# Cross-attention's mask carried in the last feature row of its keys, with the query weights folded on TensorE

## The chip, the core and the metric

The kernel runs on one core of a Trainium2 chip, as one launch. The metric is the device time of that launch in microseconds (us). The text calls the engines by the profile's names: PE (TensorE matmuls; PEld is its weight load), DVE (VectorE), ACT (ScalarE), POOL (GpSimd) and SP (SyncE, which here only issues DMAs).

## The reference

Four blocks run one after the other on x of shape (8, 256, 128) and ctx_512 of shape (8, 64, 64). L0 is a gated cross-attention, L1 a cross-attention with a residual, L2 six layers of a decoder, L3 a cross-attention whose softmax runs over the queries. L2 takes nearly all of the time, and the change is in it:

```python
H, D, FF, L = 16, 64, 512, 6            # heads, head size, hidden size, layers

def _ln(x, g, b, eps=1e-05):
    m = jnp.mean(x, axis=-1, keepdims=True)
    v = jnp.mean(jnp.square(x - m), axis=-1, keepdims=True)
    return (x - m) / jnp.sqrt(v + eps) * g + b

def _mha(s, t, kv_w, q_w, o_w, o_b, mask):
    k, v = jnp.split(s @ kv_w, 2, axis=-1)
    q = t @ q_w
    k, v, q = (_heads(k), _heads(v), _heads(q))
    scores = jnp.einsum('bhqd,bhkd->bhqk', q, k) * D ** (-0.5)
    scores = jnp.where(mask[:, None] == 0, jnp.float32(-1000000000.0), scores)
    attn = jax.nn.softmax(scores, axis=-1)
    o = jnp.einsum('bhqk,bhkd->bhqd', attn, v)
    ...
    return o @ o_w + o_b

def step(t, p):                          # one layer; t is (8, 256, 128)
    tn = _ln(t, norm_g, norm_b)
    t = _mha(tn, tn, skv, sq, sow, sob, tgt_mask) + t      # mask (8, 256, 256)
    tn = _ln(t, norm_g, norm_b)
    t = _mha(src, tn, ckv, cq, cow, cob, src_mask) + t     # src = ctx_512, mask (8, 1, 64)
    tn = _ln(t, pg, pb)
    return t + (jax.nn.relu(tn @ w1 + b1) @ w2 + b2), None
```

The cross-attention's mask has one row of 64 keys per batch element, the same for every head and query. norm_g and norm_b (128 values each) are the same in all layers.

## The kernel before

All of x stays in SBUF as `t`, tokens on the partitions. Work is written as steps that are put into a plan with `at(tick, phase, fn)`. At the end the steps run in order of tick and phase, and a dependency between successive instructions of PE, DVE, ACT and POOL pins each engine to that order; DMAs on SP are issued in program order. Matmul results and scores go through a rotation of four PSUM buffers of two banks each (`two_banks`, `mm_tile`, `tp_tile`); the n-th taker waits until the (n-4)-th is read out.

A layer has 32 ticks of self-attention (four per batch element b) and then 16 ticks of cross-attention (two per b, one for each half, `qt`, of the queries). The feed-forward of a b comes some ticks behind its cross-attention.

- `ahead` prepares a b's normalised input: moments on DVE, rstd on POOL, xn (on ACT at L868 if `on_scalar`, else on DVE at L873), a transpose on PE (L882), and an ACT copy to `tT` that multiplies by the column `g` and adds the column `bias` (L884; features are on the partitions there). For self-attention and cross-attention the two columns are norm_g and norm_b. Self-attention passes `on_scalar=False`.
- `plan_sa` does self-attention: projections (L902, L921), scores (L939), the exponent's input with the mask on DVE (L953), exp on ACT (L958), division on POOL (L968), transposes on DVE (L978), values (L994), output projection (L1012), addition into t (L1019).
- `plan_ca_weights` turns a layer's cross-attention weights once. It transposes w_ckv and w_cq on DVE in blocks of 32 (L1057), stores each to DRAM in four DMAs and fetches it back, regroups the first on POOL (L1074), and folds them into `AT` (keys' weights by query weights, L1083 on PE, copied by ACT) and `WVO` (values' weights by output weights, same lines).
- `plan_ca` makes the keys of two b's at once from `AT` and the context (`keys_both`: L1120 on PE, four copies on ACT, L1126). The keys are laid out as features on 128 partitions by 16 heads by 64 keys. Its scores are in `plan_weights_64`.
- `plan_weights_64` is shared with L0. For cross-attention, `scores` issues four times four matmuls of the keys (L356), and behind each four of them four bf16 matmuls that add the mask by a row of ones (L363). `lower` then copies to SBUF on ACT (L372), takes the maximum on DVE (m, L374) and subtracts it on POOL (L375); `exps` is on ACT; `divide` sums on DVE (L385) and multiplies on POOL (L387); `turn` transposes on DVE (L395); `sums` multiplies by the values on PE (L429); `add` adds into t on DVE (L1145).

These calls place the steps of `plan_ca_weights`; its `T` is six ticks ahead of the layer's cross-attention:

```python
        for i in range(2):
            at(T - 6 + i, 8.7, lambda i=i: turned(i))
            at(T - 4 + i, -0.5, lambda i=i: fetched(i))
        at(T + 1, 8.05, regrouped)
        at(T + 2, 3.6, folded("AT", 0, lambda c: st[1][:, :, c, :], HD ** -0.5))
        at(T + 3, 3.6, folded("WVO", 1, lambda c: W["ca", l][2][:, c, :]))
```

Of the kernel before, what the change touches and what calls it, by code (L numbers as in the profile page):

```python
# [8 lines left out]
F32 = mybir.dt.float32  # L9
I32 = mybir.dt.int32  # L10
BF16 = mybir.dt.bfloat16
# [16 lines left out]
def tile_xattn_stack(ctx: ExitStack, tc: tile.TileContext, io, out: bass.AP):  # L28
# [28 lines left out]
    def big(tag, bufs=4, shape=(P, 1024), dtype=F32):  # L57

        return heap.tile(list(shape), dtype, tag=tag, name=uniq(tag), bufs=bufs)
# [202 lines left out]
        return nm  # L262


    nm2 = const.tile([P, B, M], BF16, tag="nm2", name="nm2")
    nc.vector.memset(nm2, 0.0)
    ones0 = const.tile([P, 32], BF16, tag="ones0", name="ones0")
    nc.vector.memset(ones0, 0.0)
    nc.vector.memset(ones0[0:1], 1.0)


    def stats(xin, eps):
# [21 lines left out]
    def at(tick, phase, fn):  # L294
        plan.setdefault(tick, []).append((phase, fn))
# [30 lines left out]
        )  # L326
        return vw

    def plan_weights_64(tick, qt, qT, keys, values, mask, take):

        tl = {}

        def scores():
            sc = two_banks("sc").rearrange("p (q x) -> p q x", q=4)
            if mask is None:
                for i in range(4):
                    for a in range(4):
                        q = (i + 2 * (a // 2)) % 4  # L340
                        rows = slice(64 * (a // 2), 64 * (a // 2) + 64)
                        qb = 4 * qt + q
                        nc.tensor.matmul(
                            sc[32 * a : 32 * a + 32, q, :],
                            lhsT=qT()[rows, qb * 32 : (qb + 1) * 32],
                            rhs=keys()[rows, 4 * (a % 2) : 4 * (a % 2) + 4, :].rearrange(
                                "p h k -> p (h k)"
                            ),
                            start=True, stop=True,
                        )  # L350
                tl["sc"] = sc.rearrange("p q x -> p (q x)")
                return
            for q in range(4):
                qb = 4 * qt + q
                for a in range(4):
                    nc.tensor.matmul(  # L356
                        sc[32 * a : 32 * a + 32, q, :],
                        lhsT=qT()[:, qb * 32 : (qb + 1) * 32],
                        rhs=keys()[:, a].rearrange("p h k -> p (h k)"),
                        start=True, stop=False,  # L360
                    )
                for a in range(4):
                    nc.tensor.matmul(  # L363
                        sc[32 * a : 32 * a + 32, q, :], lhsT=ones0, rhs=mask,
                        start=False, stop=True,
                    )
            tl["sc"] = sc.rearrange("p q x -> p (q x)")

        def lower():
            sc = tl.pop("sc")  # L370
            e = big("e", shape=(P, 16, M))
            nc.scalar.copy(e.rearrange("p h k -> p (h k)"), sc)  # L372
            m = sm([P, 16], "m16")
            nc.vector.tensor_reduce(m, e, AX.X, ALU.max)  # L374
            nc.gpsimd.tensor_tensor(  # L375
                e, e, m.unsqueeze(2).to_broadcast([P, 16, M]), ALU.subtract
            )
            tl["e"] = e

        def exps():  # L380
            nc.scalar.activation(tl["e"], tl["e"], AF.Exp)

        def divide():
            r = sm([P, 16], "r16")
            nc.vector.tensor_reduce(r, tl["e"], AX.X, ALU.add)  # L385
            nc.vector.reciprocal(r, r)  # L386
            nc.gpsimd.tensor_tensor(  # L387
                tl["e"], tl["e"], r.unsqueeze(2).to_broadcast([P, 16, M]), ALU.mult
            )

        def turn():
            e = tl.pop("e").rearrange("p (q h) (k x) -> p (h k) q x", q=4, x=32)
            eT = big("k" if mask is None else "o", shape=(P, 8, 4, 32))
            for i in range(2):
                nc.vector.transpose(eT[:, 4 * i : 4 * i + 4], e[:, 4 * i : 4 * i + 4])  # L395
            tl["eT"] = eT

        def sums_by_head():

            ps = two_banks("mm").rearrange("p (i x) -> p i x", i=2)  # L400
            eT, vw = tl.pop("eT"), values()
            for i in range(2):
                for k in range(2):
                    for j in range(4):
                        nc.tensor.matmul(
                            ps[32 * j : 32 * j + 32, i, :P],
                            lhsT=cones.rearrange("p a f -> p (a f)") if i == 0
                            else vw[:, 4 * k + j, :],
                            rhs=eT[:, 2 * j + k].rearrange("p q x -> p (q x)"),
                            start=(k == 0), stop=(k == 1),  # L410
                        )
            r = sb([P, P], "r0", 2)
            nc.vector.reciprocal(r, ps[:, 0, :P])
            tl["oT"] = sb([P, P], "o0", 3)
            nc.vector.tensor_tensor(tl["oT"], ps[:, 1, :P], r, ALU.mult)

        def outputs():
            ps = mm_tile()
            nc.tensor.matmul(
                ps[:, :D], lhsT=tl.pop("oT"), rhs=S0["wo"], start=True, stop=True  # L420
            )
            take(ps)

        def sums():
            ps = mm_tile()
            eT, vw = tl.pop("eT"), values()
            for s in range(8):
                g, r, k = s // 4, s // 2 % 2, s % 2
                nc.tensor.matmul(  # L429
                    ps[:, :D], lhsT=eT[:, s].rearrange("p q x -> p (q x)"),  # L430
                    rhs=vw[:, r, k, g, :], start=(s == 0), stop=(s == 7),
                )
            take(ps)

        at(tick, 1, scores)
        at(tick, 2, lower)
        if mask is None:
            at(tick + 1, 2.05, exps)
            at(tick + 1, 2.5, turn)
            at(tick + 2, 1.9, sums_by_head)  # L440
            at(tick + 2, 4.6, outputs)
        else:
            at(tick, 8, exps)
            at(tick + 1, 2.4, divide)
            at(tick + 2, 2.5, turn)
            at(tick + 3, 3.0, sums)
# [188 lines left out]

    def mask_keys():
        mi = big("q", dtype=I32)
        mi = mi[0:1, : B * M].rearrange("p (b m) -> p b m", b=B)
        nc.sync.dma_start(out=mi, in_=io["mask_Bx1xS2_if1"].rearrange("b o m -> o b m"))
        nc.vector.tensor_scalar(nm2[0:1], mi, 0.0, -BIG, ALU.is_equal, ALU.mult)  # L640

    mask_bf = []

# [39 lines left out]
    def plan_l0(b, T):  # L683
# [87 lines left out]
        at(T + 1, 3.2, make_values)  # L771
        for qt in range(QT):
            plan_weights_64(
                T + qt, qt, lambda: st["q"], lambda: st["k"], lambda: st["VW"], None,
                lambda ps, qt=qt: add(qt, ps),
            )
        at(T + 3, 6, moments)
# [113 lines left out]
    def plan_sa(l, b, T):  # L891
# [134 lines left out]
        def mask():  # L1026
            st["nm"] = load_mask(b)

        ahead(b, (T - 6, 8.3), (T - 5, 2.6), (T - 5, 7.2), norm_g, norm_b, st, False)
        at(T - 2, -1, mask)  # L1030
        at(T - 4, 3.6, lambda: project(W["sa", l][2], "q", HD ** -0.5, 0, False))
        at(T - 4, 3.7, lambda: project(W["sa", l][2], "q", HD ** -0.5, 1, False))
# [13 lines left out]
    def plan_ca_weights(l, T):  # L1046
# [19 lines left out]
        def fetched(i):  # L1066
            w = W["ca", l][i]
            nc.sync.dma_start(out=w, in_=W.pop(("cab", l, i)).rearrange("j b i x -> (j b) (i x)"))
            st[i] = w.rearrange("p (i c x) -> p i c x", i=4, x=32)
# [26 lines left out]
                st[name] = res  # L1096
            return fn

        for i in range(2):
            at(T - 6 + i, 8.7, lambda i=i: turned(i))  # L1100
            at(T - 4 + i, -0.5, lambda i=i: fetched(i))
        at(T + 1, 8.05, regrouped)
        at(T + 2, 3.6, folded("AT", 0, lambda c: st[1][:, :, c, :], HD ** -0.5))
        at(T + 3, 3.6, folded("WVO", 1, lambda c: W["ca", l][2][:, c, :]))

    keys_of = {}

    def plan_ca(l, b, T):
# [3 lines left out]
        def keys_both():  # L1112
# [16 lines left out]
                    )  # L1129
            keys_of[b], keys_of[b + 1] = res  # L1130

        def make_values():
            st["VW"] = values_of(b, fold["WVO"])

        def res():
            st["tb"] = residual(b, W["ca", l][3])

        ahead(b, (T - 4, 6), (T - 3, 2.95), (T - 2, 2.9), norm_g, norm_b, st)
        if b % 2 == 0:
            at(T - 2, 3.7, keys_both)  # L1140
        at(T + 2, 3.2, make_values)
        at(T + 2, 7, res)

        def add(qt, ps):
            nc.vector.tensor_add(t[:, QT * b + qt, :], ps[:, :D], st["tb"][:, qt, :])  # L1145

        for qt in range(QT):
            plan_weights_64(
                T + qt, qt, lambda: st["tT"], lambda: keys_of[b], lambda: st["VW"],
                nm2[:, b].unsqueeze(1).to_broadcast([P, 4, M]), lambda ps, qt=qt: add(qt, ps),  # L1150
            )

    def plan_ff(l, b, T, T_second, steps=None):
# [117 lines left out]
    for l in range(NL):  # L1271
        T_ca = T0 + 4 * B
        T_next = T_ca + 2 * B
        for b in range(B):
            plan_sa(l, b, T0 + 4 * b)
        plan_ca_weights(l, T_ca - 6)
        for b in range(B):
            plan_ca(l, b, T_ca + 2 * b)
            T_ff = T_ca + 2 * b + 7
# [101 lines left out]
```

## Time and profile before

| | before |
|---|---|
| median of 3 runs | 2409.77 us (2405.57 to 2410.28) |
| profiled execution | 2410.29 us, of which the profile's span is 2408.5 |
| granted TensorE clock, mean | 0.987 |
| instructions | 100346 |
| busy: PE, DVE, ACT, POOL | 2325.2, 1872.3, 1707.7, 1359.1 us |
| chain that ended last | PE 75%, DVE 13%, ACT 5%, POOL 4% |
| L356, L363 (cross-attention's scores, mask) | 217.0 us busy in 3072, 112.4 in 1536 |
| DMA | 76.90 MB, mean 32 GB/s |

A busy share is an average over stages with different limits, and matmuls overlap, so a busy time of PE is more than the time by which it delays what follows. In the rows of the groups, the columns are line, engine, operation, output <- inputs, shape, count, then busy us and mean ns of one, then idle time of the engine just before and what ended it. In a timeline, the columns are start and duration in us, engine, line, operation, count; a bracket gives the engine's idle time before it and what released it.

### The profile page before, as it was taken

Reading aid. Unit: us, or ns where it says so; the run is one execution under the profiler, and the core shown is the slowest. Engines: PE = TensorE matmul, PEld = TensorE weight load, DVE = VectorE, ACT = ScalarE, POOL = GpSimd, SP = SyncE. Lnnn points to the kernel's source line nnn. Section 1 sums busy time; section 2 is a strip of 40 time slices with the busy share of each in tenths; the row PEclk is TensorE's granted clock in tenths of the full one; section 3 lists DMA queues with packets and bytes.
Section 4 is the critical chain, followed back from the end, with each engine's and each line's share of the span. In section 5 each row is a group of like instructions: output and inputs, shape, how many; then the busy total and the mean of one; then the engine's idle time right before and its main releaser. Section 6 shows DMA issues by size and latency. Waiting matters only on the chain.

```text
span 2408.5 us, 100346 instructions
## 1 busy us (share of the span) xinstructions
PE 2325.2 (97%) x42564; PEld 1719.9 (71%) x42564; DVE 1872.3 (78%) x6237; ACT 1707.7 (71%) x4514; POOL 1359.1 (56%) x2231
## 2 busy tenths in 40 slices
PE   7889999999999999999999999999999999999997
PEld 4557777777777777777777777777777777777775
DVE  5677887777888767888767888767888767888775
ACT  4567777667777667778667778667778667777663
POOL 2444556754556754555764555755555765455665
PEclk9989999999999999999999999999999999999998
DMA  6000022001022001012000012000013000001000
GB/s 180 2 2 20 21 73 65 2 3 30 21 64 66 11 3 30 21 56 73 12 2 26 21 45 87 12 2 18 25 40 89 21 2 18 25 26 42 2 4 16
DMA packets 102834, 76.90 MB, mean 32 GB/s; under 512 B 8113, under 2 KB 96881, under 8 KB 102386
## 3 DMA queue, kind: packets, MB, share of 16 engines
q1 hardware_dynamic: 101794, 70.16, 10.1%
q8 instruction: 335, 5.49, 0.9%
q14 instruction: 113, 0.93, 0.1%
q10 hardware_dynamic: 592, 0.33, 0.1%
HBM read 62.07 MB, written 8.39 MB: 29 GB/s over the span
## 4 chain that ended last, share of the span: by engine, by line
PE 75%; DVE 13%; ACT 5%; POOL 4%; issue 2%; DMA 0%; SPq 0%; POOLq 0%; ACTq 0%; DVEq 0%
PE sc L939 12%; PE mm L902 12%; PE mm L994 12%; PE mm L1012 6%; PE mm L921 6%; PE mm L429 6%; PE sc L356 5%; DVE e L953 3%; PE mm L1178 3%; PE mm L1161 3%; DVE eTc L978 2%; DVE m L374 2%; POOL e L968 2%; PE mm L1120 2%; PE mm L318 2%
## 5 line engine op out<-in xcount | busy, mean ns | idle before, releaser
L968 POOL TENSOR_SCALAR e<-e,rs 128x256 f32<-128x256 f32 x1536 | 702.8, 478 | 706.3 <-DVE rs L966 696.5
L958 ACT ACTIVATE e<-e,mn 128x256 f32<-128x256 f32 x1536 | 758.6, 495 | 151.3 <-DVE mn L953 146.5
L953 DVE CUSTOM_DVE_ANT_0 e<-sc,nm 128x256 f32<-128x256 f32 x1536 | 543.1, 419 | 93.4 <-PE sc L939 92.3
L978 DVE STREAM_TRANSPOSE eTc<-e 128x512 f32<-128x512 f32 x768 | 516.2, 694 | 59.4 <-POOL e L968 58.2
L939 PE MATMUL sc<-k,q 64*32 64x256 f32 x12288 | 380.8, 383 | 2.3 <-DVE o L299 1.3
L994 PE MATMUL mm<-eTc,v 32*64 32x256 f32 x12288 | 363.4, 378 | 5.7 <-ACT AT L1095 3.3
L375 POOL TENSOR_TENSOR e<-e,m 128x1024 f32<-128x1024 f32 x112 | 213.0, 1902 | 262.1 <-DVE m L374 262.1
L994 PEld LDWEIGHTS mm<-eTc,v 32*64 32x64 f32 x12288 | 277.1, 131 | 88.5 <-issue 22.2
L939 PEld LDWEIGHTS sc<-k,q 64*32 64x32 f32 x12288 | 221.8, 107 | 125.3 <-issue 51.4
L374 DVE TENSOR_REDUCE m<-e 128x16 f32<-128x1024 f32 x112 | 136.3, 1217 | 197.0 <-ACT e L372 197.0
L958 ACT ACTIVATION_READ_ACCUMULATOR e<-e,mn 128x1 f32 x1536 | 287.9, 187 | 0.0
L356 PE MATMUL sc<-q,tT 128*32 128x256 f32 x3072 | 217.0, 382 | 3.8 <-DVE t L1019 3.2
L429 PE MATMUL mm<-v,o 128*128 128x128 f32 x1536 | 197.5, 283 | 1.9 <-DVE t L1145 1.7
L429 PEld LDWEIGHTS mm<-v,o 128*128 128x128 f32 x1536 | 183.1, 195 | 19.0 <-issue 9.1
L902 PE MATMUL mm<-tT,w_sk 128*128 128x256 f32 x768 | 189.2, 389 | 0.2 <-PE mm L994 0.2
L1012 PEld LDWEIGHTS mm<-w_sow,o 128*128 128x128 f32 x1536 | 175.1, 192 | 17.6 <-issue 12.3
L921 PE MATMUL mm<-w_sv,tT 128*32 128x256 f32 x3072 | 185.6, 382 | 0.0
L1012 PE MATMUL mm<-w_sow,o 128*128 128x128 f32 x1536 | 183.6, 278 | 1.3 <-ACT WVO L1093 1.3
L387 POOL TENSOR_TENSOR e<-e,r 128x1024 f32<-128x1024 f32 x96 | 182.6, 1902 | 0.5 <-DVE r L386 0.5
L301 ACT COPY v<-mm 128x1024 f32<-128x1024 f32 x96 | 97.1, 1012 | 115.4 <-PE mm L921 115.4
L902 PE MATMUL mm<-tT,w_sq 128*128 128x256 f32 x768 | 173.6, 379 | 0.0
L902 PEld LDWEIGHTS mm<-tT,w_sk 128*128 128x128 f32 x768 | 138.3, 190 | 44.2 <-issue 29.2
(222 smaller groups left out, 3489.4 us busy)
## 6 DMA issues: line engine op xcount, KB each, us to landing
nm<-mask_d SPq DMA_DIRECT2D x192, 128.0 KB
wd<-o SPq DMA_DIRECT2D x48, 128.0 KB
w_sk<-in_L_sa_kv_dram SPq DMA_DIRECT2D x6, 512.0 KB
w_sv<-in_L_sa_kv_dram SPq DMA_DIRECT2D x24, 128.0 KB
w_sq<-in_L_sa_q_dram SPq DMA_DIRECT2D x6, 512.0 KB
w_sow<-in_L_sa_ow_dram SPq DMA_DIRECT2D x6, 512.0 KB
w_ckv<-in_L_ca_kv_dram SPq DMA_DIRECT2D x12, 256.0 KB
w_cq<-in_L_ca_q_dram SPq DMA_DIRECT2D x6, 512.0 KB
```

Source lines behind the costliest of these rows:

```text
L356: nc.tensor.matmul(sc[32 * a : 32 * a + 32, q, :], lhsT=qT()[:, qb * 32 : (qb + 1) * 32], rhs=keys()[:, a].rearrange("p h k -> p (h k)"), ...
L375: nc.gpsimd.tensor_tensor(e, e, m.unsqueeze(2).to_broadcast([P, 16, M]), ALU.subtract)
L429: nc.tensor.matmul(ps[:, :D], lhsT=eT[:, s].rearrange("p q x -> p (q x)"), rhs=vw[:, r, k, g, :], start=(s == 0), stop=(s == 7),)
L902: nc.tensor.matmul(ps[:, i * S : (i + 1) * S], lhsT=w[:, c * P : (c + 1) * P], rhs=st["tT"], start=True, stop=True,)
L921: nc.tensor.matmul(ps[32 * a : 32 * a + 32, i, :], lhsT=st["tT"][:, kb * 32 : (kb + 1) * 32], rhs=sv[:, a].rearrange("p g x -> p (g x)"), ...
L939: nc.tensor.matmul(sc[32 * a : 32 * a + 32, r, j, :], lhsT=st["q"][g][rows, a, qb * 32 : (qb + 1) * 32], rhs=st["k"][g][rows, a, :], start ...
L953: nc.vector.tensor_tensor_reduce(e[:, i, :], sc4[:, i, :], st["nm"][:, 2 * jj + i % 2, :], -1.0, 3.0 * BIG, ALU.add, ALU.min, mn[:, i : i ...
L958: nc.scalar.activation(e[:, i, :], e[:, i, :], AF.Exp, scale=-1.0, bias=mn[:, i : i + 1], accum_out=rs[:, i : i + 1],)
L968: nc.gpsimd.tensor_scalar(e[:, i, :], e[:, i, :], rs[:, i : i + 1], 1.0, ALU.mult, ALU.mult)
L978: nc.vector.transpose(eT[:, r, :, 2 * jj : 2 * jj + 2, :], e[:, 2 * r : 2 * r + 2, :].rearrange("p j (k x) -> p k j x", x=32),)
L994: nc.tensor.matmul(ops[a // 2][r * HD : (r + 1) * HD, a % 2, :S], lhsT=st["v"][kb // 4][rows, kb % 4, (2 * g + r) * HD : (2 * g + r + 1) * ...
L1012: nc.tensor.matmul(st["ps"][:, j * D : (j + 1) * D], lhsT=st["oT"][c // 4][:, c % 4, j * P : (j + 1) * P], rhs=sow[:, c, :], start=(c == 0 ...
```

## The change

Cross-attention's queries are normalised rows. Their 128 features sum to zero before norm_g and norm_b are applied, so the last feature is minus the sum of the others and need not be carried. The changed kernel uses that feature's row for a constant: `ahead` for cross-attention takes the columns `last_off` (1, and 0 in the last row) and `last_on` (0, and 1 in the last row) as scale and bias, so that row 127 of tT is 1. norm_g, norm_b and the missing feature are multiplied into the query weights by a 128x128 matrix, `to_rows`, that is made once at the start; `queries` does this with eight matmuls per layer, and they turn the weights at the same time, in place of a DVE transpose with four stores and a fetch. The last row of the keys then holds norm_b's contribution to the scores, and `mask_keys` adds the mask to it, once per b, on DVE (rows 96 to 127, of which only the last has a mask that is not zero). The mask matmuls are gone. The steps of `plan_ca_weights` start a tick earlier, and the `AT` fold with them; the `WVO` fold stays. The self-attention of the first two batch elements of a layer normalises on ACT.

```diff
-    nm2 = const.tile([P, B, M], BF16, tag="nm2", name="nm2")
-    nc.vector.memset(nm2, 0.0)
-    ones0 = const.tile([P, 32], BF16, tag="ones0", name="ones0")
-    nc.vector.memset(ones0, 0.0)
-    nc.vector.memset(ones0[0:1], 1.0)
+    nm2 = const.tile([P, B, M], F32, tag="nm2", name="nm2")
+    last_on = ident[:, P - 1 : P]
+    last_off = const.tile([P, 1], F32, tag="last_off", name="last_off")
+    nc.vector.tensor_scalar(last_off, last_on, -1.0, 1.0, ALU.mult, ALU.add)
+    to_rows = const.tile([D, D], F32, tag="to_rows", name="to_rows")
+    g_last = const.tile([D, 1], F32, tag="g_last", name="g_last")
+    nc.vector.tensor_mul(g_last, norm_g, last_on)
+    nc.vector.tensor_scalar(to_rows, ident, norm_g, g_last, ALU.mult, ALU.subtract)
+    nc.vector.tensor_copy(to_rows[:, D - 1 : D], norm_b)
+    last_big = const.tile([P, 1], F32, tag="last_big", name="last_big")
+    nc.vector.tensor_scalar(last_big, last_on, -BIG, None, ALU.mult)
...
                         lhsT=qT()[:, qb * 32 : (qb + 1) * 32],
                         rhs=keys()[:, a].rearrange("p h k -> p (h k)"),
-                        start=True, stop=False,
-                    )
-                for a in range(4):
-                    nc.tensor.matmul(
-                        sc[32 * a : 32 * a + 32, q, :], lhsT=ones0, rhs=mask,
-                        start=False, stop=True,
+                        start=True, stop=True,
                     )
...
     def mask_keys():
         mi = big("q", dtype=I32)
-        mi = mi[0:1, : B * M].rearrange("p (b m) -> p b m", b=B)
-        nc.sync.dma_start(out=mi, in_=io["mask_Bx1xS2_if1"].rearrange("b o m -> o b m"))
-        nc.vector.tensor_scalar(nm2[0:1], mi, 0.0, -BIG, ALU.is_equal, ALU.mult)
+        mi = mi[:, : B * M].rearrange("p (b m) -> p b m", b=B)
+        nc.sync.dma_start(
+            out=mi, in_=io["mask_Bx1xS2_if1"].rearrange("b o m -> (b o) m").partition_broadcast(P)
+        )
+        nc.vector.tensor_scalar(nm2, mi, 0.0, last_big, ALU.is_equal, ALU.mult)
...
-        ahead(b, (T - 6, 8.3), (T - 5, 2.6), (T - 5, 7.2), norm_g, norm_b, st, False)
+        ahead(b, (T - 6, 8.3), (T - 5, 2.6), (T - 5, 7.2), norm_g, norm_b, st, b < 2)
...
-        for i in range(2):
-            at(T - 6 + i, 8.7, lambda i=i: turned(i))
-            at(T - 4 + i, -0.5, lambda i=i: fetched(i))
+        def queries():
+            w = W["ca", l][1]
+            ps = two_banks("mm")
+            for c in range(HC):
+                cols = slice(c * P, c * P + P)
+                nc.tensor.matmul(ps[:, cols], lhsT=w[:, cols], rhs=to_rows, start=True, stop=True)
+            nc.scalar.copy(w, ps)
+            st[1] = w.rearrange("p (c d) -> p c d", c=HC)
+
+        at(T - 6, 8.7, lambda: turned(0))
+        at(T - 4, -0.5, lambda: fetched(0))
+        at(T, 3.6, queries)
         at(T + 1, 8.05, regrouped)
-        at(T + 2, 3.6, folded("AT", 0, lambda c: st[1][:, :, c, :], HD ** -0.5))
-        at(T + 3, 3.6, folded("WVO", 1, lambda c: W["ca", l][2][:, c, :]))
+        at(T + 2, 3.6, folded("AT", 0, lambda c: st[1][:, c, :], HD ** -0.5))
+        at(T + 4, 3.6, folded("WVO", 1, lambda c: W["ca", l][2][:, c, :]))
...
+        def mask_keys():
+            last = keys_of[b][96:].rearrange("p a c k -> p (a c) k")
+            nc.vector.tensor_tensor(
+                last, last, nm2[96:, b].unsqueeze(1).to_broadcast([32, 16, M]), ALU.add
+            )
...
-        ahead(b, (T - 4, 6), (T - 3, 2.95), (T - 2, 2.9), norm_g, norm_b, st)
+        ahead(b, (T - 4, 6), (T - 3, 2.95), (T - 2, 2.9), last_off, last_on, st)
         if b % 2 == 0:
             at(T - 2, 3.7, keys_both)
+        at(T - 1 - b % 2, 1.9, mask_keys)
...
-                nm2[:, b].unsqueeze(1).to_broadcast([P, 4, M]), lambda ps, qt=qt: add(qt, ps),
+                False, lambda ps, qt=qt: add(qt, ps),
...
-        plan_ca_weights(l, T_ca - 6)
+        plan_ca_weights(l, T_ca - 7)
```

In `plan_weights_64` the parameter `mask` became `halves`, true for L0 alone.

## The prediction

> **What bounds the kernel now.** I read the page first (busy shares, chain), then busy time by stage of layer 1 (ticks placed by their score matmuls), then the timelines of PE, DVE, ACT and POOL over that layer; layers 0 to 5 repeat every 369 us or so.
>
> ```profile
> PE 2325.2 (97%) x42564; PEld 1719.9 (71%) x42564; DVE 1872.3 (78%) x6237; ACT 1707.7 (71%) x4514; POOL 1359.1 (56%) x2231
> ...
> PE 75%; DVE 13%; ACT 5%; POOL 4%; issue 2%; DMA 0%; SPq 0%; POOLq 0%; ACTq 0%; DVEq 0%
> ```
>
> ```profile
> core 0: us, PE busy (x) PEld busy (x) DVE busy (x) ACT busy (x) POOL busy (x), PEclk, DMA share, GB/s
> 524.00:766.00 242.00, 240.26 (x5027) 179.16 (x5029) 202.51 (x777) 189.41 (x588) 128.38 (x272) 1.00 0.15 43
> 766.00:786.00 20.00, 19.05 (x388) 13.82 (x384) 13.99 (x29) 11.67 (x20) 15.59 (x18) 1.00 0.19 51
> 786.00:808.00 22.00, 20.48 (x302) 15.03 (x298) 16.28 (x34) 12.60 (x18) 15.23 (x14) 0.92 0.01 2
> 808.00:846.00 38.00, 37.81 (x544) 29.71 (x528) 29.00 (x76) 27.66 (x49) 29.95 (x30) 1.00 0.01 2
> ```
>
> PE is full in self-attention (524 to 766) and in cross-attention from 808 on. Between 766 and 808 (ticks 0 to 6) it idles 2.5 us and has one stretch at half clock. 75% of the chain is PE, a quarter is not; the first ticks of cross-attention, which this change works on, are among that quarter. Below, "tick n" is counted from the layer's first cross-attention tick.
>
> **The change, part by part.**
>
> *Mask matmuls out.* A group of four L363 records delays the next score matmul only a little:
>
> ```profile
> 766.29 0.29 PE L363 MATMUL sc<-nm,ones 128*32 128x256 bf16 x4
> 766.40 0.61 PE L356 MATMUL sc<-q,tT 128*32 128x256 f32 x8
> ```
>
> 766.29 to 766.40 is 0.11 us, four times per tick: 0.436 us, 16 ticks per layer: 6.98, six layers: 41.9 us of PE time. (L363's busy row of 112.4 us counts overlapped time.) What it saves depends on the tick:
>
> ```profile
> 769.29 1.22 DVE L374 TENSOR_REDUCE m<-e 128x16 f32<-128x1024 f32 x1 [0.98 <-ACT e L372]
> ...
> 771.28 0.98 PE L994 MATMUL mm<-eTc,v 32*64 32x256 f32 x10 [0.40 <-DVE eTc L978]
> ...
> 785.28 0.64 PE L356 MATMUL sc<-q,tT 128*32 128x256 f32 x8 [0.55 <-DVE t L1019]
> ...
> 793.97 1.22 DVE L374 TENSOR_REDUCE m<-e 128x16 f32<-128x1024 f32 x1 [1.26 <-ACT e L372]
> ```
>
> In ticks 0 to 2 PE waits for DVE, and one loop runs m (DVE 1.22), subtract (POOL 1.90), exp (ACT 1.06), copy (ACT 1.0): PE's saving becomes idle, 0. Tick 3 gains 0.44. In ticks 4 to 6 m follows m by 5.2 to 6.1 us through the same loop: 0. In ticks 7 to 15 PE is full: 9 x 0.436 = 3.9, of which I take 3.5, since the scores of ticks 11 and 12 wait for DVE's add into t. Per layer -3.9 instead of -6.98.
>
> *Mask added to the keys.* 48 new DVE additions on rows 96 to 127, 32x1024, in ticks -1, 0, 3, 4, 7, 8, 11, 12. The trace has no such instruction. Nearest row in the groups:
>
> ```profile
> L631 DVE TENSOR_TENSOR AT<-mm,eTc 128x1024 f32<-128x1024 f32 x1 | 1.2, 1207 | 0.0
> ```
>
> and, on the timelines of DVE, ACT and POOL (start, duration, idle before and its releaser):
>
> ```profile
> 761.51 0.43 DVE L953 CUSTOM_DVE_ANT_0 e<-sc,nm 128x256 f32<-128x256 f32 x1 [1.09 <-PE sc L939]
> ...
> 759.53 2.05 ACT L1126 COPY q<-mm 128x512 f32<-128x512 f32 x4 [0.37 <-PE mm L1120]
> ...
> 46.74 1.90 POOL L375 TENSOR_TENSOR e<-e,m 128x1024 f32<-128x1024 f32 x1 [10.60 <-DVE m L374]
> ...
> 48.11 0.81 DVE L513 TENSOR_TENSOR e<-e 8x256 f32<-8x256 f32 x1
> ```
>
> L631 reads one operand from PSUM and holds DVE for about 1.14 us (successive starts of reduces of that size stand 1.14 apart). By that row an addition is 1.14. The Trainium skill (SBUF — State Buffer, section "SBUF: two separate sides") speaks against it: a DVE instruction with two SBUF inputs and a GpSimd instruction that reads SBUF take turns on an exclusive lock, each waiting out the whole other. This case's trace agrees at one spot: L513, 8x256 and both inputs in SBUF, starts at 48.11 and ends at 48.92, not before the 1.90 us POOL subtraction ends at 48.64. The additions have both inputs in SBUF, and POOL is 40 to 80% busy there. Place by place:
> - Tick -1: the addition needs the third of the four L1126 copies (about 761.1) while DVE stands ready from 760.42 and the next e starts at 761.51. Queued behind it are that exponent's four L953. Bare: +0.8; with POOL's L859 (761.14 to 761.84) in front: up to +1.5.
> - Tick 0: ahead of m is 0.98 us of idle, filled; m comes +0.2 later, and POOL, ACT and the tick 0 to 2 loop with it. This adds to the former only in part: +0.1 bare, 0 with what is already late.
> - Tick 3: m waits for ACT's copy, later anyway: 0. Tick 4: the gap before m at 793.97 is 1.26. Bare it fits, 0. With the lock it starts after POOL's L387 (791.90 to 793.80) and m comes +1.0 late, in the loop that sets ticks 4 to 6.
> - Ticks 7, 8, 11, 12: DVE is 76% busy and PE holds the path: 0 bare; in tick 11 the two L873 that go away (2.11 us at 845.12, PE idle 0.88) pay for it.
> Sum per layer: +0.9 by the nearest row, +2.5 by the rule. Bounds: 0 (all hidden), and 8 x 1.9 = 15 if every one waited a POOL instruction out on the path, which the DVE gaps exclude. I take +2.5: a spot of the trace stands behind the rule.
>
> *Query weights turned on TensorE.* `queries`, tick -7: 8 matmuls like L1012's (16 records, half of a 3.84 us group of 32, about 1.85) and one ACT copy (1.01, L301). Tick -7 is PE-bound:
>
> ```profile
> 716.36 1.96 PE L939 MATMUL sc<-k,q 64*32 64x256 f32 x64
> 718.25 3.71 PE L994 MATMUL mm<-eTc,v 32*64 32x256 f32 x128
> ```
>
> Each starts as the one before ends (the next, L902, at 721.89): +1.85. The PSUM buffer rotation gets one more taker, whose ACT copy has three later takers' time; 0. Gone are a 1.20 us DVE transpose (L1057), four stores and one fetch on SP per layer: -0.2, since PE waited 0.21 us for DVE behind it at 709.09; SP's and the DMA queues' share of the chain is 0%. The first turn, its fetch and the POOL regroup (L1074, 1.04 us) come one tick earlier, where POOL is 53% and the 16 DMA engines 15% busy (128.38 and 0.15 in the first row by stage): 0. WVO's fold stays at its tick.
>
> *AT one tick earlier.* The fold (L1083) goes from tick -4 to -5:
>
> ```profile
> 738.72 1.96 PE L939 MATMUL sc<-k,q 64*32 64x256 f32 x64
> ...
> 739.92 0.42 DVE L953 CUSTOM_DVE_ANT_0 e<-sc,nm 128x256 f32<-128x256 f32 x1 [0.59 <-PE sc L939]
> ...
> 741.44 1.97 PE L1083 MATMUL mm<-w_cq,o 64*64 64x128 f32 x32 [0.76 <-POOL o L1074]
> ```
>
> Tick -5 (731.3 to 738.7) is full of PE work, and DVE waits 0.59 for the scores that follow. From 739.92 to 760.42 DVE runs without a gap worth naming and ACT is late behind it, so taking 1.9 from tick -4's PE (which has 0.76 idle before it) gives nothing back: +1.9. Lower bound 0, if DVE's queue absorbs the delay.
>
> *Scale and bias, b<2.* Same ACT instruction for tT. The two L873 per b (562 ns) become ACT L868 (484 ns) with two small ones, in ticks 11 and 15 of the layer before: counted above; at the start two 1.18 us L873 go away that PE waited for (3.19 and 1.61 at L713): -2.2.
>
> *Start.* Five small DVE instructions need norm_g and norm_b, whose DMAs SP issues at 20.76 and 21.23. They stand in DVE's order ahead of and within the L548/L549 chain (20.98, 21.99, 23.00), which ACT, then PE follow. With about 2 us to land, an estimate, +2.9 (0 to 4). The mask's load is 256 KB instead of 2, behind 20 us of slack: 0.
>
> *Clock.* After idles in tick 6 PE ran at half clock:
>
> ```profile
> 804.60:807.90 3.30, 3.30 (x23) 2.88 (x29) 2.43 (x3) 1.73 (x3) 1.84 (x2) 0.50 0.02 5
> 1173.20:1176.50 3.30, 3.23 (x52) 2.57 (x53) 1.92 (x3) 2.33 (x5) 1.84 (x2) 1.00 0.00 0
> ```
>
> Four such windows in the run; layers 2 and 4 escape. Tick 6 takes 11.3 us with one and 10.1 without. The Trainium skill (TensorE: Matmul & The Clock Gate, section "HAM oscillation — how this bites in real kernels") asks for an idle window of some 3.4 us; here 1.20 + 0.27 us, visible idle just before, sufficed. By the page the change's longer idles (2.5 to 2.9 us) cost 0; by the trace the two layers that escaped lose up to 1.2 each: 2.4. I take +1.5 (estimate), near the trace; bounds -4.8 (all four windows gone) and +7 (one more in each layer).
>
> **Sum.** Per layer -3.9 + 2.5 + 1.85 - 0.2 + 1.9 = +2.1, six: +12.8. Start +0.7, clock +1.5: +15. The profiled execution took 2410.29 (span 2408.5 and 1.8 around it), 0.5 above the median of three: about 2425; I say 2424.
>
> **Rivals.**
> - *Bare mask.* No lock: per layer 1.6 less, +0.5; with start and clock +5: 2415.5. For it: L513 is one spot. Against: L873 varies from 305 to 1431 ns beside POOL.
> - *PE alone is the bound* (faster). The DVE additions hide, the loops of ticks 0 to 6 slide with PE, AT is absorbed in tick -4: 6.98 is saved against 1.85 - 0.2: -5.3 a layer, -32; or -4.0, -24, if ticks 4 to 6 (1.3) still gain nothing. With the start's +0.7: 2379 to 2387, about 2384. For it: 97% busy, 75% of the chain. Against: the idles shown. It decides if m's wait for ACT (0.98 to 2.04 in ticks 0 to 2) shrinks by 0.4 a tick.
> - *More half clock.* Every layer's ticks 1 and 6 fall to it, 2.4 a layer, some of it there already: 2436 to 2444.
> - The change doesn't do what it says: excluded; the instructions are there.
>
> **Numbers.** Forecast 0.45, bare 0.22, PE alone 0.25, half clock 0.08. 0.2% is 4.8 us (2405.5 to 2415.1), about what a measurement here can tell. The bare case straddles its upper end: same 0.13; slower 0.45 + 0.08 + 0.09 = 0.62; faster 0.25. Range 2384 to 2436: it leaves out half of the PE case and the last, 0.2. The slower cases' own range: 2414 to 2436.
>
> **What would show it.** Right: L1083 in tick -5 and a DVE wait for scores there near 2 us; the new DVE rows above 1.5 us where POOL runs; ticks 0 to 6 not shorter. Wrong: PE's idle between 766 and 808 unchanged and ticks 0 to 6 shorter by 0.4 each; or the additions at 0.5 us and less.

## The result and the profile after

The changed kernel takes 2425.36 us (median of 6 runs, 2424.29 to 2426.87) against 2410.03 for the kernel before, run beside it. The ratio is 1.007, with a 95% interval of 1.0059 to 1.008: 15.3 us slower. Forecast: 2424. Line numbers below are those of the changed kernel: L356 is now L366, L374 is L379, L939 is L946, L994 is L1001, L1083 is L1090, and the new addition is L1152.

The page's busy times and chain, after:

```profile
span 2424.5 us, 97478 instructions
...
PE 2308.7 (95%) x41124; PEld 1701.9 (70%) x41124; DVE 1918.4 (79%) x6269; ACT 1720.6 (71%) x4544; POOL 1396.9 (58%) x2243
...
PE 74%; DVE 14%; ACT 7%; POOL 3%; issue 1%; DMA 1%; SPq 0%; POOLq 0%; ACTq 0%; DVEq 0%
```

PE lost 16.5 us of busy time and the span grew by 16.0. The first stages of layer 1's cross-attention, which begins 5 us later than before, show where (busy by stage):

```profile
core 0: us, PE busy (x) PEld busy (x) DVE busy (x) ACT busy (x) POOL busy (x), PEclk, DMA share, GB/s
771.00:791.00 20.00, 17.55 (x312) 11.73 (x306) 15.13 (x30) 10.24 (x20) 15.12 (x16) 0.91 0.14 36
791.00:815.00 24.00, 20.33 (x254) 14.66 (x250) 19.98 (x38) 15.03 (x23) 16.34 (x16) 0.94 0.07 20
815.00:853.00 38.00, 36.72 (x467) 28.22 (x466) 33.28 (x80) 27.41 (x49) 32.66 (x31) 0.99 0.01 2
```

In the first 20 us PE is busy for 17.55 instead of 19.05, at a clock of 0.91 instead of 1.00. In the third row DVE has gone from 29.00 to 33.28 of 38 us. PE has less to do and waits more.

All ticks can be laid side by side, since each starts with its score matmuls. The table gives the change of the ticks' lengths against the kernel before, in us per layer, as a mean over six layers of one profiled execution. All figures come from the starts of L939/L946 and L356/L366 and their counterparts. The fourth column is the changed kernel without the additions; the last is the version in the last experiment. The last two rows are not per layer: they stand once in a run. The last layer's tick 15 has no next tick and is counted in the last row.

| ticks | forecast | after | without additions | combined |
|---|---|---|---|---|
| -32 to -6 (query weights) | +1.65 | +1.35 | +1.32 | +1.36 |
| -5 to -1 (AT fold) | +1.9 | +1.89 | +1.89 | +0.07 |
| 0 to 2 (with the additions of ticks -1, 0) | +1.5 | +1.64 | -0.41 | -0.41 |
| 3 | -0.44 | -0.44 | -0.44 | -0.44 |
| 4 to 6 | +1.0 | +1.25 | -0.36 | -0.39 |
| 7 to 15 | -3.5 | -3.14 | -4.23 | -3.13 |
| sum of these | +2.1 | +2.55 | -2.23 | -2.94 |
| first score of layer 0 later by | +0.7 | +1.13 | +0.85 | -2.02 |
| from the last layer's tick 15 to the end | none | -0.34 | +1.74 | -1.11 |

Six times 2.55, the start's 1.13 and the end's -0.34 make the 16 us of the span. Stretches in which the granted clock was half lie inside these rows: between 200 and 2350 us there were 4 of 3.41 us before (tick 6 of four layers) and 10 after (tick 1 of layers 1 to 5, and tick 6 of all layers but 3). The end has its own: the mean clock there is 0.86 before, 0.87 after and 0.83 without additions, so its +1.74 goes with the clock.

### The profile page after: what moved, and what is told of

It is laid out like the page before. It is cut to its first block, busy times and chain, and to the rows that moved or that the text cites. A ratio compares the mean times of both kernels' runs of the same rounds, so it can differ in the third digit from the quotient of the medians.

```text
span 2424.5 us, 97478 instructions
## 1 busy us (share of the span) xinstructions
PE 2308.7 (95%) x41124; PEld 1701.9 (70%) x41124; DVE 1918.4 (79%) x6269; ACT 1720.6 (71%) x4544; POOL 1396.9 (58%) x2243
## 4 chain that ended last, share of the span: by engine, by line
PE 74%; DVE 14%; ACT 7%; POOL 3%; issue 1%; DMA 1%; SPq 0%; POOLq 0%; ACTq 0%; DVEq 0%
PE mm L909 14%; PE sc L946 13%; PE mm L1001 13%; PE mm L1019 7%; PE mm L928 7%; PE mm L434 4%; PE sc L366 3%; PE mm L1203 3%; PE mm L1186 3%; DVE m L379 2%; DVE o L400 2%; DVE q L1152 2%; DVE e L960 2%; DVE r L390 1%; ACT e L965 1%
## 5 line engine op out<-in xcount | busy, mean ns | idle before, releaser
L1001 PE MATMUL mm<-eTc,v 32*64 32x256 f32 x12288 | 371.4, 384 | 21.4 <-DVE eTc L985 21.4
L946 PE MATMUL sc<-k,q 64*32 64x256 f32 x12288 | 379.9, 382 | 1.5 <-ACT v L311 0.6
L1001 PEld LDWEIGHTS mm<-eTc,v 32*64 32x64 f32 x12288 | 282.8, 134 | 107.1 <-issue 42.7
L946 PEld LDWEIGHTS sc<-k,q 64*32 64x32 f32 x12288 | 221.7, 107 | 122.3 <-issue 45.6
L379 DVE TENSOR_REDUCE m<-e 128x16 f32<-128x1024 f32 x112 | 136.4, 1218 | 126.1 <-ACT e L377 125.4
L366 PE MATMUL sc<-q,tT 128*32 128x256 f32 x3072 | 185.5, 382 | 8.6 <-DVE t L1170 7.9
L392 POOL TENSOR_TENSOR e<-e,r 128x1024 f32<-128x1024 f32 x96 | 182.6, 1902 | 0.5 <-DVE r L391 0.5
```

Of the source, the lines that this page charges most:

```text
L366: nc.tensor.matmul(sc[32 * a : 32 * a + 32, q, :], lhsT=qT()[:, qb * 32 : (qb + 1) * 32], rhs=keys()[:, a].rearrange("p h k -> p (h k)"), ...
L946: nc.tensor.matmul(sc[32 * a : 32 * a + 32, r, j, :], lhsT=st["q"][g][rows, a, qb * 32 : (qb + 1) * 32], rhs=st["k"][g][rows, a, :], start ...
L1001: nc.tensor.matmul(ops[a // 2][r * HD : (r + 1) * HD, a % 2, :S], lhsT=st["v"][kb // 4][rows, kb % 4, (2 * g + r) * HD : (2 * g + r + 1) * ...
```

## Experiments

Times are set against the kernel before in the runs of the same job, where its median was 2408.6 to 2409.1.

**The additions.** Two kernels: one without them, which leaves cross-attention's mask out, and one in which an instruction of the same size reads a single operand.

```diff
-        at(T - 1 - b % 2, 1.9, mask_keys)
```

> The changed kernel without the 48 additions of the mask to the keys (the mask is left out; nothing else changes). Theory (the additions hold the loop of maximum, subtraction and exp in ticks -1 to 6, partly by making POOL and DVE wait for each other): 2.5 us a layer go, 15 in all, 2410, about the kernel before. Rival 'bare' (an addition costs no more than its own 1.2 us of DVE, most of it in gaps): 0.9 a layer, about 2420. Rival 'PE alone' (the additions are hidden, the loss is PE work in self-attention): no change, 2425.

Measured: 2397.05, ratio 0.9952 (0.9939 to 0.9964), 11.9 us faster than the kernel before and 28 faster than the changed one. That is nearly twice what any theory gave. The additions are the loss; everything else in the change together is a gain.

```diff
-            nc.vector.tensor_tensor(
-                last, last, nm2[96:, b].unsqueeze(1).to_broadcast([32, 16, M]), ALU.add
-            )
+            nc.vector.tensor_reduce(last, last.unsqueeze(3), AX.X, ALU.add)
```

> The changed kernel with each of the 48 additions turned into a DVE instruction of the same size, place, output and dependencies that reads the keys alone (a sum over an axis of length 1; the mask is not added). Theory (DVE and POOL lock each other out when the DVE instruction has two SBUF inputs): the instructions take 1.2 us each with none at 2.15, POOL's rstd in tick -1 takes 0.7 and not 1.8, and the time lies between the changed kernel and the one without additions: about 2416, 5 to 6 us above the latter. Rival (it is the DVE time and the order of the queue that cost, not the lock): as the changed kernel, 2425, within 2 us.

Measured: 2413.46, ratio 1.002 (1.0013 to 1.0027). It lies between, 12 us below the changed kernel and 16 above the one without additions, where the theory had 5 to 6. The line's instructions, min/median/max in ns, first after, then here:

```profile
L1152 DVE TENSOR_TENSOR q<-q,nm x48: 1221/1222/2152, 395.8 to 2345.0; 32x1024 f32<-32x1024 f32 x48
```

```profile
L1152 DVE TENSOR_REDUCE q<-q x48: 1215/1216/1218, 392.3 to 2330.2; 32x1024 f32<-32x1024 f32 x48
```

With one SBUF input no instruction is late in 48; with two, 12 take 2.15 us, 0.93 more, and 5 take 1.82. All 17 started while POOL's multiplication L392 was running. The timelines of POOL and DVE of the changed kernel show who came first:

```profile
798.55 1.90 POOL L392 TENSOR_TENSOR e<-e,r 128x1024 f32<-128x1024 f32 x1
...
799.38 2.15 DVE L1152 TENSOR_TENSOR q<-q,nm 32x1024 f32<-32x1024 f32 x1
...
766.38 1.22 DVE L1152 TENSOR_TENSOR q<-q,nm 32x1024 f32<-32x1024 f32 x1 [0.71 <-ACT q L1144]
...
766.40 1.77 POOL L866 TENSOR_TENSOR rstd<-ve,mhalf 128x2 f32<-128x2 f32 x1
```

At 799.38 POOL's multiplication holds until 800.45 and DVE ends 1.08 us after that. At 766.38 DVE is ahead, and POOL's 128x2 power, which takes 0.70 elsewhere and never over 0.71 in one_input, takes 1.77. So the two wait for each other here, both ways, as the forecast had it. It does not hold for every POOL instruction, though: at 2306.62 an addition starts 0.03 us after such a power had begun; it takes 1.25, the power 0.69.

In ticks 4 to 6 this lock is the price: one_input shows -0.52 there, against +1.25 after and -0.36 without additions. Of that 1.77, 0.93 is tick 5, in every layer alike; most of the rest is tick 6, at half clock in five layers after and in one in one_input. In ticks 0 to 2 the lock is none of it (+1.62 against +1.64; in the layers without half clock +1.16 against +1.17), nor in ticks 11 and 12 (-1.25 against -1.24). There the queue is the price:

```profile
774.47 1.22 DVE L1152 TENSOR_TENSOR q<-q,nm 32x1024 f32<-32x1024 f32 x1
775.72 1.22 DVE L379 TENSOR_REDUCE m<-e 128x16 f32<-128x1024 f32 x1
776.86 1.29 DVE L985 STREAM_TRANSPOSE eTc<-e 128x512 f32<-128x512 f32 x2
...
777.71 5.77 PE L1001 MATMUL mm<-eTc,v 32*64 32x256 f32 x128 [2.45 <-DVE eTc L985]
```

This is the addition of tick 0 in layer 1. DVE has no gap before it; m and then the transposes stand behind it, and PE waits 2.45 us for them instead of 0.40. PE's next group then runs at half clock (5.77 us instead of 4.21; granted clock of the stretch 0.52):

```profile
777.90:781.30 3.40, 3.40 (x65) 2.02 (x71) 1.56 (x8) 2.34 (x4) 1.92 (x3) 0.52 0.00 0
```

The same wait doesn't always bring half clock. It is there in all six layers, and layer 0 escapes:

```profile
407.10 4.21 PE L1001 MATMUL mm<-eTc,v 32*64 32x256 f32 x128 [2.45 <-DVE eTc L985]
```

In layer 0 ticks 0 to 2 are 1.17 longer than before, in the five others 1.51 to 1.82. So the queue costs 1.6 of the 2.05 that lie between the columns "after" and "without additions", and half clock the rest.

**Place.** All additions moved: those of the first two elements behind tick -1's exponent inputs and ahead of tick 1's maximum, the others pairwise ahead of the maximum of ticks 3, 7 and 11.

```diff
-        at(T - 1 - b % 2, 1.9, mask_keys)
+        if b < 2:
+            at(*((T - 1, 2.15) if b == 0 else (T - 1, 1.9)), mask_keys)
+        else:
+            at(T - 1 - 2 * (b % 2), 1.9 + 0.01 * (b % 2), mask_keys)
```

> The changed kernel with all 48 additions kept but moved into gaps of DVE: for the first two batch elements of a layer, behind the eight exponent inputs of tick -1 and ahead of the maximum of tick 1 (where DVE idles 1.7 us); for the others, both of a pair ahead of the maximum of the tick in which their keys are ready (ticks 3, 7, 11; gaps of 2.3 to 3.5 us before). Theory (the place costs, not the work): half to all of the additions' price goes, 2411 to 2418. Rival (their number and the lock cost wherever they stand): 2425, within 3 us.

Measured: 2422.99, ratio 1.0059 (1.0046 to 1.0071), a gain of some 2 us: the rival's outcome, but not for its reason. By ticks, 0 to 2 went from +1.64 to +0.70 and 4 to 6 from +1.25 to -0.46, as the theory has it; ticks 11 and 12 went from -1.24 to +0.67 and 7 to 10 from -0.75 to -0.36. Two additions in a row in a tick in which DVE has no gap, with half clock in tick 12 of three layers, took back what the others gave.

**The AT fold.** Put back in the changed kernel, and brought forward in the kernel before (there with its turns and fetches a tick earlier as well):

```diff
-        at(T + 1, 8.05, regrouped)
-        at(T + 2, 3.6, folded("AT", 0, lambda c: st[1][:, c, :], HD ** -0.5))
+        at(T + 2, 8.05, regrouped)
+        at(T + 3, 3.6, folded("AT", 0, lambda c: st[1][:, c, :], HD ** -0.5))
```

> The changed kernel with the regrouping of the keys' weights and the AT fold put back one tick later, the fold at tick -4 as before; everything else as changed. Theory (tick -5 is bound by PE, ticks -4 to -1 by DVE and ACT, where PE idles about 3 us after the change): 1.9 us a layer come back, 11.4, so 2414. Rival (what comes back is lost again to the copies of AT and WVO on ACT, which then stand close together): 2420 to 2425.

> The kernel before with one part alone: the turns, fetches and regrouping of the cross-attention's weights and the AT fold one tick earlier, the fold at tick -5. Theory (1.9 us of PE work enter a tick bound by PE and leave one that is not): 11 us slower, 2419 to 2421; without half-clock effects 11.3. Rival (the price that undoing it in the changed kernel showed, 15.5, is the fold's whole price): 2424.

Measured: 2409.82, ratio 1.0008 (1.0 to 1.0017), and 2417.18, ratio 1.0037 (1.0025 to 1.005). Undone it gives back 15.5, done alone it costs 8.1. By ticks both agree with 1.9: rows -5 to -1 are 0.00 and +1.90. Most of the rest is half clock, inferred from the counts: at_late has 6 stretches between 200 and 2350 us instead of 10, before_at_early 2 instead of 4. In before_at_early tick -9 gives back 1.7 us as well: it is 0.28 shorter in each layer. PE's timeline after shows the step as forecast, the fold without idle time in tick -5, and idle time at the next values; DVE waits 2.48 us there for the scores (until 745.19) instead of 0.59:

```profile
742.09 1.96 PE L1090 MATMUL mm<-w_cq,o 64*64 64x128 f32 x32
743.98 3.68 PE L946 MATMUL sc<-k,q 64*32 64x256 f32 x128
748.80 1.57 PE L1001 MATMUL mm<-eTc,v 32*64 32x256 f32 x27 [1.13 <-DVE eTc L985]
```

**The mask matmuls alone.** The kernel before without them, so that cross-attention's mask is left out:

```diff
-                        start=True, stop=False,
-                    )
-                for a in range(4):
-                    nc.tensor.matmul(
-                        sc[32 * a : 32 * a + 32, q, :], lhsT=ones0, rhs=mask,
-                        start=False, stop=True,
-                    )
+                        start=True, stop=True,
+                    )
```

> The kernel before with only its mask matmuls taken out (the mask is left out of cross-attention; nothing else changes). Forecast's step: 3.9 us a layer saved, 23 in all, 2386 (0 in ticks 0 to 2 and 4 to 6). Rival A (the saving is nearly the whole 0.436 us in all ticks): 42 us, 2367. Rival B, from the changed kernel without additions (eight ticks gain 0.44, the others nothing; the rest of its gain in tick 11 came from the normalisation moved to ACT): 3.5 us a layer, 2388.

Measured: 2390.9, ratio 0.9923 (0.9911 to 0.9936), 17.8 us. Less than half of the 41.9 us of PE time comes off the time. Per layer, ticks 0 to 2 gain 0.41, one tick's worth where the forecast had none; ticks 7 to 15 gain 2.81 instead of 3.5. Ticks 4 to 6 gain nothing: their +0.30 is tick 6, now at half clock in all six layers instead of four. From the last layer's tick 15 to the end the run is 1.84 us longer, at a mean clock of 0.83 instead of 0.86.

**Normalising the first two elements on ACT.** Undone in the changed kernel, and done alone in the kernel before:

```diff
-        ahead(b, (T - 6, 8.3), (T - 5, 2.6), (T - 5, 7.2), norm_g, norm_b, st, b < 2)
+        ahead(b, (T - 6, 8.3), (T - 5, 2.6), (T - 5, 7.2), norm_g, norm_b, st, False)
```

> The changed kernel with the normalisation of the first two batch elements' self-attention back on DVE (b<2 becomes False), all else as changed. Forecast's step: worth about as much as the addition of tick 11, and 2.2 us at the start, so 2428 to 2430. Rival (it is what makes tick 11 two us shorter in the changed kernel without additions, and the additions of ticks 11 and 12 then have no gap): 1.6 us a layer and 2.2 at the start, 2434 to 2438.

> The kernel before with one part of the change alone: the self-attention of a layer's first two batch elements normalises on ACT. Forecast's step: 2.2 us at the start and next to nothing in the layers, 2406 to 2407. Rival, from undoing it in the changed kernel (21 us slower): 1.6 us in tick 11 of five layers, more where a stretch at half clock goes with it, and the start: 2390 to 2399.

Measured: 2446.62, ratio 1.016 (1.0147 to 1.0174), and 2400.53, ratio 0.9967 (0.9955 to 0.9979). Alone it is worth 8.6 us, undone beside the additions 21. In the kernel before it shortens tick 11 by 1.58 in five layers and brings the first score 2.03 earlier. With DVE's xn back in the changed kernel, ticks 11 and 12 go from -1.24 to +1.27. PE waits, and in three layers it then runs its scores at half clock (3.16 us instead of 1.93):

```profile
858.01 0.30 PE L889 MATMUL tp<-ident,xn 128*128 128x128 f32 x1 [2.37 <-DVE xn L880]
...
858.86 3.16 PE L366 MATMUL sc<-q,tT 128*32 128x256 f32 x32
```

**Towards a better version.** Three attempts, all with AT later (tick -4, in the second -3), POOL adding for the first two elements in tick -1, and the third and fourth on DVE ahead of tick 3's maximum. They differ in the query weights' place and in the seventh addition. The second and third cuts show only what they change beside the first.

```diff
+        dt, ph = [(-1, 1.9), (-3, 1.91), (-1, 1.9), (-3, 1.91), (-1, 1.9), (-2, 1.9),
+                  (-1, 2.55), (-2, 1.9)][b]
+        at(T + dt, ph, mask_keys)
...
+            (nc.gpsimd if b < 2 else nc.vector).tensor_tensor(
```

> The changed kernel with the AT fold back at tick -4, and the additions kept but spread: those of the first two batch elements on POOL in tick -1, where it idles 3.4 to 5 us; the next two both ahead of the maximum of tick 3; the others on DVE as changed but for the seventh, which goes behind the transposes of tick 11. Theory (place, lock and tick of the fold are what cost): 15 us for the fold (measured), and of the additions' 28 us the share of ticks -1 to 6, some 18 to 24: 2386 to 2394, faster than the kernel before. Rival (POOL's additions are slower and hold its reciprocals and divisions): 2400 to 2410.

```diff
-        at(T, 3.6, queries)
+        at(T + 3, 3.6, queries)
...
-        at(T + 2, 3.6, folded("AT", 0, lambda c: st[1][:, c, :], HD ** -0.5))
-        at(T + 4, 3.6, folded("WVO", 1, lambda c: W["ca", l][2][:, c, :]))
+        at(T + 4, 3.6, folded("AT", 0, lambda c: st[1][:, c, :], HD ** -0.5))
+        at(T + 5, 3.8, folded("WVO", 1, lambda c: W["ca", l][2][:, c, :]))
```

> As spread_late, and also the query weights' matmuls moved from tick -7 (PE-bound) to tick -4, the AT fold to tick -3 and the WVO fold to tick -2, where PE idles. Theory: 1.8 us a layer of PE time in tick -7 come back, and ticks -4 to -1 hide them: 11 us faster than spread_late, 2376 to 2384. Rival (ACT, whose copies of the three results and of the keys then stand in three successive ticks, becomes late; the keys wait for AT): no faster than spread_late, or up to 10 us slower.

```diff
-            at(T - 2, 3.7, keys_both)
+            at(T - 2 - (b == 6), 3.7, keys_both)
...
-                  (-1, 2.55), (-2, 1.9)][b]
+                  (-2, 1.9), (-2, 1.9)][b]
```

> As spread_late, but the last pair's keys are made one tick earlier (tick 9), and the seventh element's addition goes ahead of the maximum of tick 10, where DVE idles 2.2 us and POOL 1.9. Theory (the addition behind the transposes of tick 11 waits for POOL and holds that tick's scores, 1.9 us a layer): 11 us faster than spread_late's 2405.6, 2393 to 2397, faster than the kernel before. Rival (tick 11 is bound otherwise, by the sum into t): within 3 us of spread_late.

Measured: 2405.64, ratio 0.9992 (0.9985 to 0.9999); 2405.31, 0.9981 (0.9972 to 0.9989); 2406.13, 0.999 (0.9982 to 0.9998). In spread_late ticks 0 to 2 and 4 to 6 lose most of their price (+0.33 and -0.16, against -0.41 and -0.36 without additions), but the seventh addition, behind the transposes of tick 11, waits for POOL and holds the scores (ticks 11 and 12 at -0.25 instead of -2.19 without additions). In spread_slack, the query weights' 1.8 us left tick -7 and came back as +2.19 in ticks -5 to -1: there was no slack to put them in. In spread_keys tick 11 went the rival's way: ticks 11 and 12 rose to +0.56, with half clock in tick 12 of three layers. What binds them there was not shown.

**Combined.** As spread_late, with the second addition ahead of tick 1's maximum, the seventh as in the changed kernel, and the start's three instructions put off:

```diff
+        dt, ph = [(-1, 1.9), (-1, 1.9), (-1, 1.9), (-3, 1.91), (-1, 1.9), (-2, 1.9),
+                  (-1, 1.9), (-2, 1.9)][b]
+        at(T + dt, ph, mask_keys)
...
+            (nc.gpsimd if b == 0 else nc.vector).tensor_tensor(
...
+        at(15, 5.9, make_rows)      # g_last, to_rows and the copy of norm_b
         at(15, 6, mask_keys)
```

> The version that the runs point to, with the whole of the reference's work: the changed kernel with the AT fold at tick -4; the additions of a layer's first element on POOL in tick -1, of the second ahead of the maximum of tick 1, of the third and fourth ahead of that of tick 3, of the others as changed; and the three start instructions that wait for norm_g and norm_b put off to the end of the first stage. Theory, by the steps measured so far: from spread_late's 2405.6 some 0.6 us a layer in tick 1, 0.9 in tick 11 and 2.9 at the start (the forecast's figure for those three): 2393 to 2398, faster than the kernel before with the normalisation alone (2400.5). Rival (the steps' savings fall into stretches at half clock, as in spread_keys, and the start's chain waits for something else): 2401 to 2406.

Measured: 2388.64 (2387.19 to 2389.42), ratio 0.9914 (0.99 to 0.9928): 19.9 us faster than the kernel before, and faster than the lower end that was expected. Two stretches at half clock remain within the layers (at 433.5 and 798.7 us), where the kernel before has 4 and the changed one 10. The start's step is seen on DVE's timeline, first after, then here:

```profile
23.50 0.16 DVE L275 TENSOR_TENSOR g_last<-L_norm_g,ident 128x1 f32<-128x1 f32 x1 [3.12 <-DMA L_norm_g<-in_L_norm_g_dram]
...
24.43 0.47 DVE L554 SCALAR_TENSOR_TENSOR o<-mm,cg,o 64x256 f32<-64x256 f32 x1
```

```profile
21.39 0.48 DVE L557 SCALAR_TENSOR_TENSOR o<-mm,cg,o 64x256 f32<-64x256 f32 x1 [0.31 <-ACT o L556]
```

## Why the prediction was right, point by point

- *AT one tick earlier, +1.9*: measured +1.89, and the reason given (ticks -4 to -1 are not bound by PE) held in both directions.
- *Query weights, +1.85 - 0.2*: tick -7 is 1.76 longer, tick -9 0.28 shorter. The forecast put the latter down to the DVE transpose that is gone; before_at_early, which keeps both transposes but a tick earlier, shows the same 0.28, so what counted is where they stand. With a small shift at layer 0's start this makes the row's +1.35.
- *Start*: the forecast put the DVE chain 2.9 later; its first link stands at 24.43 after, against 20.98 before and 21.39 with the three instructions put off: 3.0 to 3.5. The -2.2 for xn showed as -2.03.
- *Mask matmuls, -3.9 a layer*: mis-sized, by place more than in all. Alone they give 17.8 us, 3.0 a layer. The step that failed is "in ticks 7 to 15 PE is full", of which 3.5 was taken: 2.81 came. Ticks 0 to 2, put at 0, gave 0.41. The rest of the shortfall is half clock in tick 6 and at the end of the run.
- *The additions, +2.5 a layer*: mis-sized as a price, since taking them out gives 28/6 = 4.7. As a change against the kernel before, the rows of ticks 0 to 6 (+1.64, -0.44, +1.25 against +1.5, -0.44, +1.0) came near: the forecast had put the change's gains there at 0, and the additions did swallow them. Its mechanism for tick 4 (the lock, +1.0) was right: 0.93 came. For ticks -1 and 0 the time was near by luck and the reason wrong: not the late start in tick -1 and POOL's rstd, but the addition of tick 0 ahead of m, which the forecast had priced at 0.1.
- *b<2, paid for by the addition of tick 11*: mis-sized. It is worth 8.6 us alone, of which the forecast had only the start's 2.2. In tick 11 it gave 1.58 and the addition took 1.02, so it more than paid.
- *Clock, +1.5*: 10 stretches instead of 4, and too small. An estimate from the ticks' lengths: in ticks 0 to 2 the five layers with half clock are 2.8 us longer together than five like layer 0, ticks 4 and 5 are 0.6 longer there, and tick 6 is 1.5 longer in all; about 5 us.

So the sum was right partly by luck. Outside half clock a layer came out near 1.7 us longer instead of 2.1, some 2.3 us less in six, while half clock cost some 3.5 more than was put down for it. Within the layers two steps erred against each other as well: the matmuls' gain in ticks 7 to 15 was too large by 0.7 a layer, tick 11's balance, put at 0, too small by 0.5.

Of the rivals, "PE alone" is refuted by before_no_mask, "bare" by the 17 additions that took 1.82 and 2.15 us and by ticks 4 to 6. "More half clock" named the places rightly, since 10 of its 12 stretches came; at 2425 instead of 2436 to 2444 its price was wrong: a stretch in tick 1 costs some 0.6 net, since tick 1 grows by 1.4 to 1.7 and tick 2 shrinks by 1.05.

## What to carry to other kernels

Cutting PE time pays only where no other engine's loop sets the pace; so lay the starts of a repeated instruction side by side, tick by tick, before and after, and price each place rather than each instruction. An instruction that is cheap by its duration is dear ahead of others in a full in-order queue: three of the eight additions of a layer put elsewhere, the fold put back and three start instructions put off turned 15 us lost into 20 us gained. Where two engines may lock each other out, a stand-in of the same size with one operand separates the lock from the queue.

## What the runs showed of the hardware

- A DVE addition with two SBUF inputs and POOL instructions that read SBUF waited for each other, in both directions: DVE 2.15 us instead of 1.22 where POOL's multiplication was ahead, POOL's power 1.77 instead of 0.70 where DVE was. A power ahead of DVE held nothing (1.25). A one-input instruction of the same shape was never held (1215 to 1218 ns in 48).
- Idle times of PE of 2.37 and 2.45 us, the former with 0.29 behind it, could be followed by 3.41 us at half clock, but were not each time: the 2.45 stands in all six layers of the changed kernel and of at_late, and half clock followed in five and in one. So a DVE delay can cost PE a second time.
